# Token layers taken image by image, attention of one image beside the FFN of another

## The chip, the cores and the metric

The kernel runs on one core of one Trainium2 chip. The time is device microseconds (us) of an execution; four runs of the kernel before gave 10815.32 to 10830.81 us, median 10817.74. One further execution was recorded by the hardware profiler and is what the views of the profile show. Engines are named as the profile names them: PE (TensorE, matmuls and transposes; PEld is its weight load), DVE (VectorE), ACT (ScalarE), POOL (GpSimd), SP (SyncE, which issues the DMAs here). L684 is line 684 of the kernel.

## The reference

Four images of 64 x 64 pixels with 96 channels pass four layers. Layers 0 and 1 are group normalisation and a selective scan in four directions, added to x. Layers 2 and 3 treat the pixels as tokens, 4096 an image, and they are what the change rearranges:

```
t = t + attn(ln(t), Wqkv, bqkv, Wff, bff)     # layer 2, and again layer 3
t = t + ffn(ln(t), W1, b1, W2, b2)

attn(x):  q, k, v = split(x @ Wqkv + bqkv), 6 heads of 16
          y = (q @ k.T / 4) @ v               # per head, no softmax
          return y @ Wff + bff
ffn(x):   h = relu(qlinear(x, W1, b1))        # 96 -> 384
          return qlinear(h, W2, b2)           # 384 -> 96
qlinear(x, W, b) = qacc(qacc(q8(x) @ q8(W).T) + q8(b))
```

`ln` normalises each token over its 96 channels. `q8` rounds to an 8-bit float with 5 exponent and 2 mantissa bits, `qacc` to a 16-bit float. No image needs another one's data in any layer.

## The kernel before

**Scans.** A layer's four images are taken as two pairs; two layers give four units. Each unit is `scan_inputs` (projection and convolution), `scan_pair` (the selective scan, with its order written out by hand) and `scan_outputs`. `between_scans` drives the outputs of one unit and the inputs of the next in turn, as two generators; the outputs of the last unit run alone, since there is no next unit. `scan_outputs` is a loop of 16 steps, each for four groups of 128 tokens: load zt, ys and xr; statistics of ys and `ln_rs` (a power on POOL); normalise ys on ACT (L289); six transposes into the PSUM tile `pt` (L296); two ACT activations `gt<-pt` (L299); multiply by zt on DVE (L306); eight matmuls `po` (L310, L311); add xr and store x (L313, L316). `pt` and `po` have one buffer each.

**Token layers.** All four images are loaded to SBUF as `tok[b]`, tiles of 128 partitions x 32 tokens x 96 channels, and stay there. Then `attention` runs over the four images, `ffn` over the four, and both again for layer 3. Each function opens its own pools and loads its own weights at its start.

*The norm*, `token_norm`, opens both. DVE takes 32 statistics `tstats` (L684), five small operations make the variance, DVE adds epsilon (`tn_ve`, L79), POOL takes the power -0.5 of 128 x 32 values (`tn_rs`, L81), DVE makes `tshift` (L699). Then the normalised tokens `tn` are written, 24 of 32 by ACT (L705) and 8 by POOL (L703).

*Attention.* Having no softmax, it becomes one 97 x 96 matrix an image: PE sums the Gram matrix of tn with a column of ones (L754, 32 matmuls), and five small products with the weights, with DVE copies between them, give `whole` (L764). `turn_tokens` transposes tn in groups of four (`tnps`, L714), ACT copies them to `tnt`. Then for each of eight groups PE multiplies four blocks of tnt by `whole` (`ops`, L769) and DVE adds the result to the tokens (L771).

*FFN.* The same norm and turning (ACT's copy `xq` rounds to 8 bits), then eight chunks of 512 tokens. For each of three blocks of the hidden layer: a matmul `hps`, ACT copies to 16 bits (`h`, L811), DVE adds the bias and takes the maximum with 0 (`hb`, L813), POOL rounds to 8 bits (`hq`, L814). Then twelve matmuls `ops` (L818), ACT copies (`o`, L822), DVE adds the bias (`ob`, L824) and adds to the tokens (`tok`, L826). In layer 3 each image is stored to `out` at its end.

**The order of the work.** Scans are kept in program order. In the other parts the scheduler of the framework fixes the order on each engine when the program is built, from the program order, the dependences and the buffers of each pool (two as a rule, three for `hps`). Every engine and SP's queue then runs its instructions in that order, and one that waits holds up those behind it. The tokens are loaded from the DRAM tensor to which the outputs of the second scan layer store x.

Of the kernel before, what the change touches and what calls it, by code (L numbers as in the profile page):

```python
# [16 lines left out]
F32 = mybir.dt.float32  # L17
BF16 = mybir.dt.bfloat16
# [7 lines left out]
NB = 4  # L26
HW = 64
L = HW * HW
C = 96
# [74 lines left out]
def between_scans(tc, cst, ident, half, u, before, after):  # L104


    with ExitStack() as stage:
        if before is None:
            for _ in scan_inputs(tc, stage, cst, ident, half, u, *after):
                pass  # L110
        elif after is None:
            for _ in scan_outputs(tc, stage, ident, half, *before):
                pass
        else:
            ins = scan_inputs(tc, stage, cst, ident, half, u, *after)
            for _ in scan_outputs(tc, stage, ident, half, *before):
                for _ in range(2):
                    next(ins, None)
            for _ in ins:
                pass  # L120
# [126 lines left out]
def scan_outputs(tc, stage, ident, half, layer, pr):  # L247
# [4 lines left out]
    pp = stage.enter_context(tc.tile_pool(name="c_ps", bufs=1, space=PSUM))  # L252
# [3 lines left out]
    for g in range(NT // 2):  # L256
# [36 lines left out]
        pt = pp.tile([128, 3, 2, 128], F32, name="pt")  # L293
        for j, first in enumerate((0, 256, 128)):
            for t in range(2):
                nc.tensor.transpose(pt[:, j, t], ys[:, t, first : first + 128], ident)  # L296
        gt = p2.tile([128, 3, 2, 128], F32, name="gt")
        for s, js in ((0, slice(0, 2)), (1, slice(2, 3))):
            nc.scalar.activation(  # L299
                gt[:, js],  # L300
                pt[:, js],
                AF.Identity,
                bias=par[:, s, P_NB : P_NB + 1],
                scale=par[:, s, P_NW : P_NW + 1],
            )
        nc.vector.tensor_tensor(gt, gt, zt.rearrange("p j (t q) -> p j t q", q=128), ALU.mult)  # L306
        po = pp.tile([128, 2, 2, C], F32, name="po")
# [372 lines left out]
def token_norm(nc, pool, half, t, tn):  # L680

    stats = pool.tile([128, NT, 6], F32, name="tstats")
    for j in range(NT):
        nc.vector.bn_stats(stats[:, j], t[:, j])  # L684

# [13 lines left out]
    nc.vector.scalar_tensor_tensor(shift, mean2, -0.5, rs, ALU.mult, ALU.mult)  # L699
    for j in range(NT):  # L700
        scale, bias = rs[:, j : j + 1], shift[:, j : j + 1]
        if j % 4 == 3:
            nc.gpsimd.tensor_scalar(tn[:, j, :C], t[:, j], scale, bias, ALU.mult, ALU.add)  # L703
        else:
            nc.scalar.activation(tn[:, j, :C], t[:, j], AF.Identity, bias=bias, scale=scale)  # L705


def turn_tokens(nc, pp, ident, tn, out):

    n = tn.shape[2]  # L710
    for g in range(NT // 4):
        ps = pp.tile([n, 512], F32, name="tnps", tag="tp")
        for j in range(4):
            nc.tensor.transpose(ps[:, 128 * j : 128 * j + 128], tn[:, 4 * g + j], ident)  # L714
        nc.scalar.activation(out[:, 512 * g : 512 * g + 512], ps, AF.Copy, saturate=False)


def attention(tc, cst, ident, half, tok, w):


    nc = tc.nc
    with ExitStack() as stage:
        p1 = stage.enter_context(tc.tile_pool(name="t1", bufs=1))
        p2 = stage.enter_context(tc.tile_pool(name="t2", bufs=2))
        pp = stage.enter_context(tc.tile_pool(name="t_ps", bufs=2, space=PSUM))

        wkv = p1.tile([C + 1, 2 * C], F32, name="wkv")
        nc.sync.dma_start(out=wkv, in_=w["wkv"])
        wq = p1.tile([C, C + 1], F32, name="wq")
        nc.sync.dma_start(out=wq, in_=w["wq"])  # L730
        wff = p1.tile([C, C], F32, name="wff")
        nc.sync.dma_start(out=wff, in_=w["Wff"])
        bff = p1.tile([C + 1, C], F32, name="bff")
        nc.sync.dma_start(out=bff, in_=w["bff"])

        def product(a, b, name):

            ps = pp.tile([a.shape[1], b.shape[1]], F32, name=name, tag="small")
            nc.tensor.matmul(ps, a, b, start=True, stop=True)
            return ps  # L740

        def kept(ps, name):
            to = p2.tile(list(ps.shape), F32, name=name)
            nc.vector.tensor_copy(to, ps)
            return to

        for b in range(NB):
            t = tok[b]
            tn = p2.tile([128, NT, C + 1], F32, name="tn")
            nc.gpsimd.memset(tn[:, :, C : C + 1], 1.0)  # L750
            token_norm(nc, p2, half, t, tn)
            gram = pp.tile([C + 1, C + 1], F32, name="gram")
            for j in range(NT):
                nc.tensor.matmul(gram, tn[:, j], tn[:, j], start=(j == 0), stop=(j == NT - 1))  # L754
            tnt = p2.tile([C + 1, L], F32, name="tnt")
            turn_tokens(nc, pp, ident, tn, tnt)
            gk = kept(product(kept(gram, "gram"), wkv[:, :C], "gkps"), "gk")
            vk = product(wkv[:, C:], gk, "vkps")

            heads = p2.tile([C, C], F32, name="heads")  # L760
            nc.vector.tensor_tensor(heads, cst["heads"], vk, ALU.mult)
            rest = kept(product(heads, wff, "hps"), "rest")
            whole = p2.tile([C + 1, C], F32, name="whole")
            nc.vector.tensor_tensor(whole, bff, product(wq, rest, "wps"), ALU.add)  # L764
            for g in range(NT // 4):
                po = pp.tile([128, 4, C], F32, name="ops", tag="o")
                for j in range(4):
                    at = 512 * g + 128 * j
                    nc.tensor.matmul(po[:, j], tnt[:, at : at + 128], whole, start=True, stop=True)  # L769
                tg = t[:, 4 * g : 4 * g + 4]  # L770
                nc.vector.tensor_tensor(tg, tg, po, ALU.add)  # L771


def ffn(tc, ident, half, tok, w, out=None):

    nc = tc.nc
    NH = HID // 128
    with ExitStack() as stage:
        p1 = stage.enter_context(tc.tile_pool(name="f1", bufs=1))
        p2 = stage.enter_context(tc.tile_pool(name="f2", bufs=2))  # L780
        pp = stage.enter_context(tc.tile_pool(name="f_ps", bufs=2, space=PSUM))

        def quantised(shape, src, name, back=False):
            raw = p1.tile(shape, F32, name=name)
            nc.sync.dma_start(out=raw, in_=src)
            q = p1.tile(shape, E5M2, name=name + "q")
            nc.vector.tensor_copy(q, raw, saturate=False)
            if back:
                nc.vector.tensor_copy(raw, q)
                return raw  # L790
            return q

        w1 = quantised([C, HID], w["W1"], "w1")
        w2 = quantised([128, NH, C], w["W2"].rearrange("(k p) c -> p k c", p=128), "w2")
        b1 = quantised([128, NH], w["b1"], "b1", back=True)
        b2 = quantised([128, 1, C], w["b2"].unsqueeze(0).partition_broadcast(128), "b2", back=True)

        for b in range(NB):
            t = tok[b]
            tn = p2.tile([128, NT, C], F32, name="tn")  # L800
            token_norm(nc, p2, half, t, tn)
            xq = p2.tile([C, L], E5M2, name="xq")
            turn_tokens(nc, pp, ident, tn, xq)
            for c in range(L // 512):
                cols = slice(512 * c, 512 * c + 512)
                hq = p2.tile([128, NH, 512], E5M2, name="hq")
                for k in range(NH):
                    ps = pp.tile([128, 512], F32, name="hps", tag="mm", bufs=3)
                    nc.tensor.matmul(ps, w1[:, 128 * k : 128 * k + 128], xq[:, cols], start=True, stop=True)
                    h = p2.tile([128, 512], F16, name="h16")  # L810
                    nc.scalar.copy(h, ps)  # L811
                    hb = p2.tile([128, 512], F16, name="hb16")
                    nc.vector.tensor_scalar(hb, h, b1[:, k : k + 1], 0.0, ALU.add, ALU.max)  # L813
                    nc.gpsimd.tensor_copy(hq[:, k], hb, saturate=False)  # L814
                po = pp.tile([128, 4, C], F32, name="ops", tag="o")
                for j in range(4):
                    for k in range(NH):
                        nc.tensor.matmul(  # L818
                            po[:, j], hq[:, k, 128 * j : 128 * j + 128], w2[:, k], start=(k == 0), stop=(k == NH - 1)
                        )  # L820
# [6 lines left out]
            if out is not None:  # L827
                nc.sync.dma_start(out=out[b * L : (b + 1) * L, :].rearrange("(p j) c -> p j c", j=NT), in_=t)
# [164 lines left out]
```

## Time and profile before

| what | us |
|---|---|
| median of four runs | 10817.74 |
| profiled execution, its own time | 10834.03 |
| its span (first to last instruction) | 10832.2 |
| scans with the three stages between them, up to | 10137 |
| outputs of the last unit, alone | 10137 to 10263 (126) |
| attention, layer 2, four images | 10263 to 10377 (114) |
| FFN, layer 2 | 10377 to 10546 (169) |
| attention, layer 3 | 10546 to 10654 (108) |
| FFN, layer 3, with the last store | 10654 to 10832 (178) |

The profiled execution stands 0.15% above the median. Over the whole span DVE is busy 90%, POOL 83%, ACT 81% and PE 75% of the time, but that is an average over the scans, which fill 94% of it; the tail after 10137 us is 695 us with other limits. In the views, a line gives the start, the busy time, the engine, the line of the kernel, out<-in with shapes, how many instructions it joins, and in brackets the idle time before it and what ended that. The columns of a table by windows are the busy time of each engine (with the number of its instructions), the granted clock of PE as a share of full speed, the share of the DMA engines' time, and GB/s.

### The profile page before, as it was taken

The numbers are of one execution on the slowest core, as the hardware profiler recorded it, in microseconds if no ns is written. First come the engines' busy times: TensorE is split into PE (matmuls) and PEld (weight loads), VectorE is DVE, ScalarE is ACT, GpSimd is POOL, SyncE is SP. The second block draws the span as 40 slices with busy tenths as digits, with TensorE's granted clock in tenths as the row PEclk, the third lists the DMA queues.
The fourth block names the chain that finished last, engine by engine and source line by source line (L and its number), as shares of the span: only waits on it lengthen the run. The fifth ranks groups of instructions, "written<-read, shape, count | busy, mean of one in ns | idle before, by whom it ended". The sixth has DMA issues, their size and how long they took to land. (4 is left out here: it accounts for less than half of the span.)

```text
span 10832.2 us, 143079 instructions
## 1 busy us (share of the span) xinstructions
PE 8093.1 (75%) x48032; PEld 5988.3 (55%) x48032; DVE 9706.9 (90%) x6962; ACT 8760.8 (81%) x18679; POOL 9006.5 (83%) x5242
## 2 busy tenths in 40 slices
PE   7777777777777777776877777777777777777666
PEld 4555555554555555555555555555455555555544
DVE  7999999997999999998799999999699999999655
ACT  6888888885888888886688888888588888888556
POOL 3999999992899999996598999999299999999544
PEclk9889899888899888988898999988888989898766
DMA  4677777775677777777576777777467777777600
GB/s 124 205 209 214 214 224 216 215 219 141 201 209 211 217 214 217 218 214 194 149 210 207 214 218 220 220 216 216 134 206 210 213 215 221 219 215 214 185 3 25
DMA packets 960471, 2114.16 MB, mean 195 GB/s; under 512 B 413526, under 2 KB 704664, under 8 KB 762008
## 3 DMA queue, kind: packets, MB, share of 16 engines
q1 hardware_dynamic: 959736, 2105.01, 68.0%
q8 instruction: 381, 6.24, 0.3%
q14 instruction: 354, 2.90, 0.1%
HBM read 1943.27 MB, written 161.48 MB: 194 GB/s over the span
## 5 line engine op out<-in xcount | busy, mean ns | idle before, releaser
L71 POOL TENSOR_TENSOR h<-h,cb 128x1024 f32<-128x1024 f32 x3072 | 7201.2, 2368 | 277.7 <-issue 77.2
L71 DVE TENSOR_TENSOR_SCAN h<-da,last,bp 128x1024 f32<-128x1024 f32 x2064 | 4735.1, 2334 | 131.7 <-PE bp L71 14.4
L71 ACT ACTIVATE x<-dut,bt 128x128 f32<-128x128 f32 x12288 | 3494.9, 369 | 1.8 <-PE bp L71 1.2
L71 PE MATMUL yp<-ident,h 128*128 128x128 f32 x24576 | 3343.0, 296 | 9.8 <-POOL h L71 9.8
L71 PEld LDWEIGHTS yp<-ident,h 128*128 128x128 f32 x24576 | 3170.2, 156 | 127.7 <-issue 77.2
L71 ACT ACTIVATE da<-delta,amat 128x1024 f32<-128x1024 f32 x2752 | 3063.6, 1138 | 183.4 <-DVE h L71 183.0
L71 PE MATMUL bp<-ident,x 128*128 128x128 f32 x10240 | 1655.7, 313 | 1305.9 <-DVE h L71 928.6
L71 PEld LDWEIGHTS bp<-ident,x 128*128 128x128 f32 x10240 | 1338.2, 161 | 1859.0 <-ACT x L71 1045.0
L71 DVE TENSOR_TENSOR bp<-du,bp 128x1024 f32<-128x1024 f32 x1472 | 1778.6, 1212 | 244.2 <-PE bp L71 242.5
L71 DVE TENSOR_TENSOR_SCAN h<-da,bp 128x1024 f32<-128x1024 f32 x688 | 1537.5, 2274 | 48.1 <-ACT da L71 8.5
L71 PE MATMUL bp<-bparts,sel 96*128 96x512 bf16 x2944 | 921.1, 395 | 839.8 <-DVE h L71 816.2
L71 PEld LDWEIGHTS <-sel 96*128 96x128 bf16 x2944 | 224.7, 100 | 1648.7 <-DVE h L71 1037.4
L71 ACT ACTIVATE bp<-delta,amat 128x1024 f32<-128x1024 f32 x320 | 358.1, 1119 | 542.3 <-DVE h L71 540.7
L71 POOL TENSOR_TENSOR dbu<-du,bb 128x1024 f32<-128x1024 f32 x320 | 755.9, 2362 | 0.0
L71 POOL TENSOR_TENSOR du<-delta,u 128x1024 f32<-128x1024 f32 x192 | 506.7, 2639 | 199.6 <-ACT delta L71 172.7
L81 POOL TENSOR_TENSOR ln_rs<-ln_ve,half 128x4 f32<-128x4 f32 x64 | 84.0, 1312 | 594.4 <-DVE ln_ve L79 494.3
L71 DVE TENSOR_TENSOR_SCAN h<-bp,last,dbu 128x1024 f32<-128x1024 f32 x240 | 558.4, 2327 | 13.4 <-POOL dbu L71 12.3
L71 PE MATMUL xps<-u,wx 128*76 128x512 f32 x768 | 559.5, 818 | 5.7 <-ACT cdt L71 2.9
L71 POOL COPY last<-h 128x2 f32<-128x2 f32 x1152 | 225.2, 195 | 401.1 <-DVE h L71 398.4
L71 ACT ACT_TABLE_LOAD x384 | 492.7, 1283 | 6.9
L71 PE MATMUL dps<-cdt,wdt 12*128 12x512 f32 x768 | 450.2, 667 | 0.0
L71 ACT COPY dut<-dups 128x512 f32<-128x512 f32 x384 | 220.8, 575 | 251.6 <-PE dups L71 251.6
(132 smaller groups left out, 6444.9 us busy)
## 6 DMA issues: line engine op xcount, KB each, us to landing
cb<-crow SPq DMA_DIRECT2D x1024, 1024.0 KB
cb<-crow SPq DMA_DIRECT2D x1024, 512.0 KB
bb<-crow SPq DMA_DIRECT2D x384, 256.0 KB
bb<-crow SPq DMA_DIRECT2D x128, 512.0 KB
y<-ysum SPq DMA_DIRECT2D x192, 256.0 KB
kept<-y SPq DMA_DIRECT2D x160, 256.0 KB
y<-ysum SPq DMA_DIRECT2D x64, 512.0 KB
zt<-zg SPq DMA_DIRECT2D x64, 384.0 KB
```

Of the source, the lines that this page charges most:

```text
L71: return self.tc.keep_in_program_order(getattr(self.engine, op)(*args, **kwargs))
L81: nc.gpsimd.tensor_tensor(rs, ve, half, ALU.pow)
```

## The change

The pools of the token layers are opened once, in a new function `token_layers`, which also drives the last unit's `scan_outputs`. `attention` and `ffn` become generators for one image, with a `yield` after every eight statistics, after the norm, after every eight tn and after every group or chunk; the turning of tokens is done group by group, inside the loops. `together` advances its pieces one `yield` each in turn. The order of the pieces is written out: the last outputs with the first image's layer-2 attention; seven stages of one FFN and one attention of different images; the last FFN alone. All weights of both layers are loaded ahead of the last outputs, `tok0` and `tok1` too, `tok2` and `tok3` after them.

PSUM is shared out anew: Gram and the small products have one bank each (two before), `hps` two (three before), and the outputs use the banks of `hps` and `ops`. In `scan_outputs`, at every one of its four uses, `pt` becomes two tiles of three transposes, in two buffers, and `gt` takes four activations instead of two, half as wide. `sel` and `ident16` move to a pool that ends with the scans, so that their load stands behind the load of the layers' parameters.

```
-        pt = pp.tile([128, 3, 2, 128], F32, name="pt")
-        for j, first in enumerate((0, 256, 128)):
-            for t in range(2):
-                nc.tensor.transpose(pt[:, j, t], ys[:, t, first : first + 128], ident)
         gt = p2.tile([128, 3, 2, 128], F32, name="gt")
-        for s, js in ((0, slice(0, 2)), (1, slice(2, 3))):
-            nc.scalar.activation(gt[:, js], pt[:, js], AF.Identity, ...)
+        for t in range(2):
+            pt = pp.tile([128, 3, 128], F32, name="pt", tag=turned)
+            for j, first in enumerate((0, 256, 128)):
+                nc.tensor.transpose(pt[:, j], ys[:, t, first : first + 128], ident)
+            for s, js in ((0, slice(0, 2)), (1, slice(2, 3))):
+                nc.scalar.activation(gt[:, js, t], pt[:, js], AF.Identity, ...)
...
     for j in range(NT):
         nc.vector.bn_stats(stats[:, j], t[:, j])
+        if j % 8 == 7:
+            yield
...
     nc.vector.scalar_tensor_tensor(shift, mean2, -0.5, rs, ALU.mult, ALU.mult)
+    yield
     for j in range(NT):
...
+        if j % 8 == 7:
+            yield
...
+def attention(nc, pool, pp, cst, ident, half, t, w):
...
+    tn = pool.tile([128, NT, C + 1], F32, name="tn", bufs=3)
+    nc.gpsimd.memset(tn[:, :, C : C + 1], 1.0)
+    yield from token_norm(nc, pool, half, t, tn)
+    gram = pp.tile([C + 1, C + 1], F32, name="gram", bufs=1)
+    tnt = pool.tile([C + 1, L], F32, name="tnt")
     for g in range(NT // 4):
+        for j in range(4 * g, 4 * g + 4):
+            nc.tensor.matmul(gram, tn[:, j], tn[:, j], start=(j == 0), stop=(j == NT - 1))
+        turn_tokens(nc, pp, ident, tn, g, tnt)
+        yield
...
+def ffn(nc, pool, pp, ident, half, t, w, out=None):
...
+    tn = pool.tile([128, NT, C + 1], F32, name="tn", bufs=3)
+    yield from token_norm(nc, pool, half, t, tn)
+    xq = pool.tile([C, L], E5M2, name="xq")
+    for c in range(L // 512):
+        turn_tokens(nc, pp, ident, tn, c, xq)
+        yield
...
+        yield
...
+def token_layers(tc, cst, ident, half, x, outputs, a):
...
+        load(0)
+        load(1)
+        wa = [weights(attention_weights, n, ("wq", "wkv", "Wff", "bff")) for n in (2, 3)]
+        wf = [weights(ffn_weights, n, ("W1", "b1", "W2", "b2")) for n in (2, 3)]
...
+        def together(*pieces):
+            pieces = list(pieces)
+            while pieces:
+                for one in list(pieces):
+                    if next(one, pieces) is pieces:
+                        pieces.remove(one)
+
+        together(scan_outputs(tc, stage, ident, half, *outputs, pp, "mm", "o"), attend(0, 0))
+        load(2)
+        load(3)
+        together(feed(0, 0), attend(0, 1))
+        together(attend(1, 0), feed(0, 1))
+        together(feed(1, 0), attend(1, 1))
+        together(feed(1, 1), attend(0, 2))
+        together(feed(0, 2), attend(0, 3))
+        together(attend(1, 2), feed(0, 3))
+        together(feed(1, 2), attend(1, 3))
+        together(feed(1, 3))
```

## The prediction

> **What bounds the kernel now.** I read the windows of the tail first, since the scans before 10137 us keep their order, then the timeline inside one stage of each kind. Windows by stage (busy us of each engine, granted PE clock, DMA share, GB/s): last outputs; attention, FFN of layer 2; attention, FFN of layer 3.
>
> ```profile
> core 0: us, PE busy (x) PEld busy (x) DVE busy (x) ACT busy (x) POOL busy (x), PEclk, DMA share, GB/s
> 10137.00:10263.00 126.00, 72.78 (x353) 60.66 (x352) 52.27 (x192) 50.42 (x97) 16.12 (x16) 0.69 0.60 164
> 10263.00:10377.00 114.00, 83.55 (x672) 81.78 (x672) 50.18 (x227) 51.72 (x128) 35.20 (x40) 0.78 0.13 50
> 10377.00:10546.00 169.00, 100.38 (x608) 55.31 (x608) 106.90 (x304) 116.48 (x256) 106.69 (x132) 0.60 0.00 1
> 10546.00:10654.00 108.00, 82.50 (x672) 80.66 (x672) 47.88 (x213) 51.73 (x128) 35.20 (x40) 0.80 0.01 3
> 10654.00:10832.00 178.00, 99.36 (x608) 55.47 (x608) 110.14 (x320) 116.39 (x256) 106.73 (x132) 0.61 0.09 38
> ```
>
> No engine is busy over 75% of a stage: the tail is chains with engines waiting, 569 us for eight (attention, FFN) pairs of one image, 71.1 us a pair. Engine time that could lie beside other time is there. What matters is which stretches the new order lays side by side. The norm that opens each attention and FFN, in the timeline (start, us, engine):
>
> ```profile
> 10266.30 5.36 DVE L684 BATCH_NORM_STATS2 tstats<-tok 128x6 f32<-128x96 f32 x33 [3.05 <-DMA x<-xo]
> ...
> 10272.88 5.43 POOL L81 TENSOR_TENSOR tn_rs<-tn_ve,half 128x32 f32<-128x32 f32 x1 [6.18 <-DVE tn_ve L79]
> ...
> 10278.70 8.70 ACT L705 ACTIVATE tn<-tok,tshift,tn_rs 128x96 f32<-128x96 f32 x24 [20.10 <-DVE tshift L699]
> ```
>
> A norm is a chain over three engines: statistics, a power, the writing of tn. Before, most norms lie beside the previous image's main part. The main part of an FFN, VectorE alone:
>
> ```profile
> 10800.55 0.35 DVE L813 TENSOR_SCALAR hb<-h,b 128x512 f16<-128x512 f16 x1 [9.29 <-ACT h L811]
> ...
> 10812.13 0.54 DVE L826 TENSOR_TENSOR tok<-tok,ob 128x384 f32<-128x384 f32 x1
> 10812.59 0.95 DVE L813 TENSOR_SCALAR hb<-h,b 128x512 f16<-128x512 f16 x2
> 10813.65 0.78 DVE L824 TENSOR_TENSOR ob<-o,b 128x384 f16<-128x384 f16 x1
> 10814.35 0.70 DVE L813 TENSOR_SCALAR hb<-h,b 128x512 f16<-128x512 f16 x1
> 10814.97 0.54 DVE L826 TENSOR_TENSOR tok<-tok,ob 128x384 f32<-128x384 f32 x1
> ...
> 10825.61 0.56 DVE L826 TENSOR_TENSOR tok<-tok,ob 128x384 f32<-128x384 f32 x1
> ```
>
> One chunk of 512 tokens takes 2.84 us (tok at 10812.13 and 10814.97) with VectorE hardly idle: what attention adds there to VectorE comes on top. The clock, on attention's 16-matmul groups of two images:
>
> ```profile
> 10303.38 3.73 PE L769 MATMUL ops<-whole,tnt 97*128 97x96 f32 x16 [3.90 <-DVE whole L764]
> ...
> 10333.96 1.95 PE L769 MATMUL ops<-whole,tnt 97*128 97x96 f32 x16
> ```
>
> The same work takes 3.73 or 1.95 us. Last, the outputs loop, 6.85 us a step (10177.68 to 10184.53), a chain PE, ScalarE, VectorE:
>
> ```profile
> 10177.68 0.46 PE L310 MATMUL po<-wo,gt 128*128 128x96 f32 x2 [2.38 <-DVE gt L306]
> ...
> 10180.45 1.70 PE L296 MATMUL pt<-ident,ys 128*128 128x128 f32 x6
> ...
> 10182.25 1.23 ACT L299 ACTIVATE gt<-pt,par 128x512 f32<-128x512 f32 x2 [0.99 <-PE pt L296]
> 10183.52 0.96 DVE L306 TENSOR_TENSOR gt<-gt,zt 128x768 f32<-128x768 f32 x1 [1.00 <-ACT gt L299]
> 10184.53 0.46 PE L310 MATMUL po<-wo,gt 128*128 128x96 f32 x2 [2.38 <-DVE gt L306]
> ```
>
> **Part 1, outputs beside the first attention.** In the built order, token loads and 16 weight loads stand on SP ahead of the first zt load, and the whole first norm ahead of the first ys activation on ScalarE. SP: y stores end 10140.7, 16 issues of about 0.45 us (as zt's 0.48) put zt at about 10148.5, from 10143.25; hidden, because ScalarE is later. VectorE: 32 statistics (5.2 us), quantising copies and small operations bring tn_ve to about 10150.4; pow 5.43; 20 of ScalarE's tn at 8.70/24 = 0.3625 us, 7.3; with latencies first ys is at about 10163.6 against 10151.33: +12.3. In the 16 steps, attention's Gram, transposes, copies and products (PE about 25 us cold) share the engines: at worst 18, at best 0, as PE is busy 73 of 126 us. I take 10, the loop being a chain through PE. Turning in two halves lets ScalarE start after three transposes instead of six, but takes four activations for two: about -0.3 a step, -5 (0 to -10). The loop ends at 10263.3 + 12.3 + 10 - 5 = 10280.6. Attention's last eight adds stand behind the last po: 7 us (0.98 to 1.15 + 0.55 each with cold PE, some already covered). First pair stage: T0 = 10288 (10277 to 10300).
>
> **Part 2, seven pair stages.** The two pieces are driven step by step in turn, so both norms run at the same time and nothing of a main part is beside them. The built order shows it: between the last tok add of one stage and the first transposed copy of the next, VectorE has 35 to 54 (mean 47.7) of the 64 statistics, POOL two pows in a row, and ScalarE all 48 tn ahead of anything else. Priced:
> - statistics 47.7 x 0.163 (5.36/33) = 7.8
> - twelve small operations and tn_ve, six of which take about 1.0 in a norm: 1.5
> - two pows at 5.44: 10.9; tshift 0.35
> - ScalarE has written six tn beside the second pow; 42 x 0.3625 = 15.2; latency 0.1
>
> Norms: 35.8 us a stage. Their work equals before's; only its cover is gone.
>
> The main part, last tn to last tok add. First hb after about 2.0 us (xq copy 0.56, hps 0.63, h 0.56, latency). Lower pace, VectorE's: first hb to last add 25.6 (10800.55 to 10826.2), eight attention adds at 0.5 = 4.0, some 16 statistics of the next stage 2.6: 34.2. Upper, PE cold: each of eight chunks 2.4 for the FFN (three hps at 0.42, twelve ops at about 1.0 to 1.2), 1.06 for each of two sets of four transposes, 0.93 for attention's ops (3.73/4): 43.6, less 4 of transposes beside the tn writing, plus 2.0 in front and 2 behind: 43.6. Which? Rows with a clock near these stages': PE would be busy about 184/4 = 46 of 75 us, 61%, like FFN's 59% at 0.60, not attention's 73% at 0.78; but transposes and groups in a row opened it in attention. I take the middle, 38.9.
>
> The rule: the Trainium skill, "TensorE: Matmul & The Clock Gate", Part 1, says the array opens to full clock after some 3.4 us of sustained work and falls back after an idle window. By it the main part would be cold only at its start, VectorE would set the pace, and the sum below would come to about 10821. The row at 10303.38 speaks otherwise: three more groups follow at 3.62 us without a gap, up to 10318, about 15 us cold; the measurement decides, so I do not take the rule's value.
>
> P = 35.8 + 38.9 = 74.7 us a pair, against 71.1. The other edits in the pairs (one bank less for Gram, small and hps, weights loaded early) cost 0: two hps still let PE run ahead of h at 0.56, and if that cover goes, each chunk waits up to 0.4 for ScalarE, 3 us a stage, inside the cold bound. The out store of each image stands on SP beside other stages' work; no issue waits behind it.
>
> **Part 3, the last FFN alone.** Norm: 22 statistics of 32 left, 3.6; small 1.15; pow 5.44; tshift 0.35; 24 tn 8.7: 19.2. Main: 10795.1 (last tn) to 10826.2 = 31.1, less the 3.4 by which the first hb now comes sooner, its transposes no longer all ahead: 27.7. The store 6.0 as before (10826.2 to 10832.2).
>
> **Part 4, between the scans.** Three stages with the outputs' four activations, PE, VectorE and ScalarE about 97% busy there (2560 to 2600 us): 16 steps x 3 x about 0.5 us of ScalarE = 24, against the -0.3 x 48 = -14 of the earlier start; +4 (-14 to +24, the likely part -6 to +12). Scans: no instruction moves, 0; sel's load stands behind par's but is first used in the scan.
>
> **Sum.** 10288 + 7 x 74.7 + (19.2 + 27.7) + 6.0 + 4 = 10867.8 of span, +35.6 to 10832.2. The profiled execution took 10834.03, 16 above the median of 10817.74: carried over, 10853.
>
> **Rivals.**
> - *VectorE's pace (no change).* The denser stage opens the clock and main is 34.2: P = 70.0, span 10835, median 10820. For: attention's groups at 1.95. Against: FFN stages at 0.60.
> - *PE cold throughout.* Main 43.6, P = 79.4: span 10901, median 10886. For: the 15 us cold. Against: 0.78 in attention.
> - *Faster: attention rides in the gaps of VectorE.* If hb at 0.70 is slow only through POOL's hq beside it and the new spacing thins that out, the adds and statistics cost nothing and main is 2.0 + 25.6 = 27.6: P = 63.4, span 10789, median 10774. It decides from a main under 33.8, where 7 P = 487. Against: VectorE has no gap in the chunk above.
> - *The norms overlap after all*, the engines running ahead of each other: each us off the 35.8 is 7 us; it would need 5 us a stage to break even. The orders on ScalarE and POOL speak against it.
>
> **How the numbers follow.** A measurement here tells about 0.2% (21.6 us) from no change. Forecast 0.48; cold 0.19; VectorE's pace 0.19; the gaps or overlapping norms 0.14. Slower takes the forecast, the cold case and a little of VectorE's pace with T0 and the between stages at their upper bounds (12 + 8); same the rest of that and some mild overlap; faster most of the last. Range: from the early side of the gaps (main near 31.5, 10802) to the cold case with 7 us of T0's bound on it, 10893. The likeliest alone: 10835 to 10875.
>
> **What would show it.** Stages about 75 us from last tok add to last tok add; about 36 us of each without hb; two tn_rs in a row; ScalarE 48 tn in a row; first ys about 12 us later; outputs ending near 10281; main parts 35 to 43 us at a clock of 0.6 to 0.7. Wrong if a norm shows hb beside it, if main is under 34, or if the between stages move by over 15 us.

## The result and the profile after

The changed kernel takes 10847.02 us (median of 32 runs, 10830.53 to 10863.15), the kernel before, run beside it, 10824.09 us (50 runs). The ratio is 1.0021 with a 95% interval of 1.0016 to 1.0026: slower by 0.21%, 23 us.

The end of the last scan wanders by some 10 us either way from one profile to the next, though no scan instruction differs. So I compare the **tail**, from the end of POOL's last multiplication by cb (10135.86 us in the profile before, 10130.00 after) to the end of the span: 696.3 us before, 714.6 after, +18.3. The other 5 us of the +23 are not in this tail; ahead of it the kernels differ in the edit of pt between the scans and in the later load of sel and ident16, and two profiles can't show so little there.

The changed kernel's windows: last outputs with the first attention, and that attention's last adds; then, for two pair stages (an FFN and an attention driven together), the norms and the main parts (all that follows the norms); then the last FFN's norm and main part. Columns are the busy us of each engine with its instructions, the granted PE clock, DMA share and GB/s.

```profile
core 0: us, PE busy (x) PEld busy (x) DVE busy (x) ACT busy (x) POOL busy (x), PEclk, DMA share, GB/s
10130.00:10276.00 146.00, 82.73 (x471) 75.18 (x471) 61.47 (x248) 70.44 (x161) 25.86 (x27) 0.72 0.57 159
10276.00:10289.00 13.00, 12.55 (x59) 12.31 (x58) 6.06 (x18) 0.00 (x0) 0.00 (x0) 0.50 0.68 255
10289.00:10325.00 36.00, 12.74 (x65) 11.18 (x66) 10.67 (x69) 17.18 (x48) 17.39 (x19) 0.50 0.00 2
10325.00:10362.00 37.00, 30.55 (x257) 23.18 (x256) 28.48 (x82) 24.66 (x49) 16.50 (x24) 0.94 0.00 1
...
10432.00:10468.00 36.00, 12.73 (x65) 11.18 (x66) 10.51 (x67) 17.18 (x48) 17.43 (x19) 0.50 0.00 0
10468.00:10503.00 35.00, 29.11 (x257) 22.09 (x256) 25.68 (x63) 24.64 (x49) 17.02 (x24) 0.98 0.00 1
...
10790.00:10811.00 21.00, 3.50 (x12) 1.79 (x13) 4.98 (x30) 10.08 (x27) 8.66 (x9) 0.59 0.18 76
10811.00:10844.00 33.00, 19.59 (x142) 10.77 (x140) 22.03 (x40) 19.34 (x38) 16.89 (x24) 0.71 0.12 48
```

A stage falls in two halves. In the norms no engine is busy half of the 36 us; in the main part PE works at a clock of 0.94 and 0.98 and is busy over 80% of the time. The timeline of the changed kernel (start, us, engine, line), first where the last outputs start, then from the end of the first attention to the first main part:

```profile
10141.00 4.73 DVE L679 BATCH_NORM_STATS2 tstats<-tok 128x6 f32<-128x96 f32 x29 [13.64 <-DMA wq<-in_l_wq]
...
10150.58 0.36 DVE L776 CAST w1q<-w 96x384 fp8e5<-96x384 f32 x1 [4.86 <-DMA w<-in_l_W]
...
10152.63 5.43 POOL L81 TENSOR_TENSOR tn_rs<-tn_ve,half 128x32 f32<-128x32 f32 x1 [11.61 <-DVE tn_ve L79]
...
10158.37 7.27 ACT L703 ACTIVATE tn<-tok,tshift,tn_rs 128x96 f32<-128x96 f32 x20 [26.18 <-DMA zt<-zg]
...
10165.55 1.85 ACT L284 ACTIVATE ys<-ys,shift,ln_rs 128x192 f32<-128x192 f32 x4
...
10274.69 13.86 PE L763 MATMUL ops<-whole,tnt 97*128 97x96 f32 x64
...
10288.59 0.56 DVE L765 TENSOR_TENSOR tok<-tok,ops 128x384 f32<-128x384 f32 x1 [0.82 <-PE ops L763]
10289.06 8.71 DVE L679 BATCH_NORM_STATS2 tstats<-tok 128x6 f32<-128x96 f32 x54
...
10299.00 10.82 POOL L81 TENSOR_TENSOR tn_rs<-tn_ve,half 128x32 f32<-128x32 f32 x2 [32.97 <-DVE tn_ve L79]
...
10310.07 15.14 ACT L703 ACTIVATE tn<-tok,tshift,tn_rs 128x96 f32<-128x96 f32 x42 [3.09 <-DVE tshift L696]
...
10325.12 0.57 ACT L714 ACTIVATE xq<-tnps 96x512 fp8e5<-96x512 f32 x1
...
10327.55 1.18 DVE L809 TENSOR_SCALAR hb<-h,b 128x512 f16<-128x512 f16 x2 [0.78 <-ACT h L807]
```

At the start, the statistics of the first attention stop after 29 of 32, because a quantising copy stands next in VectorE's order and waits 4.86 us for its weight; the outputs' first ys waits behind the whole norm. Then the norms of the first pair: statistics, two powers, 42 tn, one behind the other. From the last add (ending 10289.15) to the first copy are 36 us in which no hb runs.

### The profile page after: what moved, and what is told of

Same layout as the page of the kernel before. It is cut to its first block, busy times and chain, and to the rows that moved or that the text cites. A ratio compares the mean times of both kernels' runs of the same rounds, so it can differ in the third digit from the quotient of the medians.

```text
span 10844.6 us, 143249 instructions
## 1 busy us (share of the span) xinstructions
PE 8058.5 (74%) x48032; PEld 5968.1 (55%) x48032; DVE 9683.7 (89%) x6962; ACT 8785.7 (81%) x18807; POOL 8997.4 (83%) x5242
## 4 chain that ended last, share of the span: by engine, by line
ACT 36%; DVE 20%; issue 19%; PE 18%; POOL 5%; DMA 1%; SPq 0%; DVEq 0%; POOLq 0%; ACTq 0%
ACT x L71 16%; ACT da L71 13%; DVE h L71 11%; PE yp L71 6%; DVE bp L71 5%; PE bp L71 5%; POOL h L71 3%; ACT bp L71 2%; PE xps L71 2%; DVE u L166 2%; PE dps L71 1%; ACT L71 1%; ACT tn L703 1%; PE cps L150 1%; PE dups L71 1%
## 5 line engine op out<-in xcount | busy, mean ns | idle before, releaser
L71 DVE TENSOR_TENSOR_SCAN h<-da,last,bp 128x1024 f32<-128x1024 f32 x2064 | 4735.1, 2334 | 130.4 <-PE bp L71 13.2
```

What stands on the lines that cost most here:

```text
L71: return self.tc.keep_in_program_order(getattr(self.engine, op)(*args, **kwargs))
```

## The experiments

The theory going in: the norms in lockstep (both at the same time, step by step) leave half of each stage bare, with no other work beside them, and whatever covers or shortens them comes off the time. The rivals: main parts and norms together would use up the engines, or the waits would only move. "To the changed kernel" below is against its 10847; each ratio is against the kernel before on the same chip.

| run | median us | ratio (95%) | tail us |
|---|---|---|---|
| kernel before | 10824.09 | 1 | 696.3 |
| changed kernel | 10847.02 | 1.0021 (1.0016 to 1.0026) | 714.6 |
| e1 split pt alone | 10830.68 | 1.0006 (0.9997 to 1.0015) | 697.4 |
| e2 offset | 10803.41 | 0.9982 (0.9973 to 0.9991) | 670.8 |
| e3 no ob | 10827.62 | 0.9998 (0.9989 to 1.0008) | 695.4 |
| e4 fewer ops | 10841.56 | 1.0016 (1.0006 to 1.0025) | 701.3 |
| e5 weights late | 10836.18 | 1.0009 (1.0000 to 1.0019) | 700.7 |
| e6 same order | 10850.57 | 1.0023 (1.0014 to 1.0032) | 711.0 |
| e7 four streams | 10788.68 | 0.9965 (0.9953 to 0.9978) | 649.6 |
| e8 power in pieces | 10839.56 | 1.0012 (1.0003 to 1.0021) | 700.5 |
| e9 square root | 10780.04 | 0.9957 (0.9945 to 0.9970) | 636.8 |
| e10 four, square root | 10682.29 | 0.9864 (0.9849 to 0.9879) | 550.3 |
| e11 before, square root | 10746.38 | 0.9929 (0.9917 to 0.9942) | 615.5 |
| e12 outputs first | 10853.12 | 1.0025 (1.0015 to 1.0036) | 724.6 |

**e1, the split of pt alone,** on the kernel before: the hunk of the change in `scan_outputs`, with two buffers for pt.

> The kernel before with the one edit of pt alone: two tiles of three transposes in two buffers, four gt activations instead of two, in all four uses of the outputs. My step 4 (+4 us in the three between stages, bounds -14 to +24) and the -5 in the last outputs: -1 us together, 10820 to 10832 at a median of 10824 for the kernel before, with the last outputs' step at about 6.5 instead of 6.85 us. Rival, read off the profiles where the scans of the changed kernel end 5.9 us earlier: the edit gains about 2 us in each between stage, and 11 us in all, 10813.

Measured 10830.68, +0.06% with an interval from -0.03 to +0.15%. The rival's -11 us falls; +4 between the scans fits, but is too small to be shown by this run alone. First ys to the end of the last xo takes 110.5 us, 111.9 before: the earlier start of gt is worth 0.1 us a step, not 0.3.

**e2, an offset of half a piece.** The pairs of the changed kernel as two streams:

```
-        together(feed(0, 0), attend(0, 1))
-        together(attend(1, 0), feed(0, 1))
...
+        offset(
+            (0, chain((feed, 0, 0), (attend, 1, 0), (feed, 1, 0), (attend, 0, 2), ...)),
+            (13, chain((attend, 0, 1), (feed, 0, 1), (attend, 1, 1), (feed, 1, 1), ...)),
+        )
```

> The changed kernel with the same pieces in the same pairs, but the second stream starts 13 yields (half a piece) after the first, so that the norm of one lies beside the main part of the other. Theory (the norms in lockstep leave 36 us of each 71.6 us stage uncovered): half a stage becomes one norm of 20 us beside a main part of 28 to 30, a stage 60, so 7 x 11.6 = 81 us less than the changed kernel, about 10770 (10735 to 10800). Rival (the engines are used up when main parts and norms lie together, or each waits in the other's order): 10830 or more.

Measured 10803.41, 44 us less than the changed kernel and less than the kernel before too: covering the norms pays, about half of the 81 worked out, and just short of the theory's bound of 10800. The timeline of this run, POOL, shows a wait that can have taken the other half:

```profile
10417.98 0.61 POOL L810 CAST hq<-hb 128x512 fp8e5<-128x512 f16 x1 [0.44 <-DVE tvar L693]
10418.78 5.43 POOL L81 TENSOR_TENSOR tn_rs<-tn_ve,half 128x32 f32<-128x32 f32 x1 [0.19 <-DVE tn_ve L79]
10424.15 0.61 POOL L810 CAST hq<-hb 128x512 fp8e5<-128x512 f16 x1
```

and VectorE:

```profile
10418.80 0.25 DVE L679 BATCH_NORM_STATS2 tstats<-tok 128x6 f32<-128x96 f32 x1
10424.24 0.57 DVE L696 SCALAR_TENSOR_TENSOR tshift<-tmean,tn_rs 128x32 f32<-128x32 f32 x1 [5.19 <-POOL tn_rs L81]
10424.73 0.34 DVE L809 TENSOR_SCALAR hb<-h,b 128x512 f16<-128x512 f16 x1
```

The power stands in POOL's order between two hq, and VectorE stands still for tshift with an hb behind it. The norm of one image stops the main part of the other for 5 us; VectorE waited 77.8 us like this in 14 norms (first table of e8). PE was hardly slower than in the changed kernel: busy 310.46 us for 2299 matmuls from 10305 to 10790 us, against 297.15 us for 2240 in its seven pair stages. How much of the missing half the wait is, this run doesn't show.

**e3 and e4, what sets the pace of the main parts.** e3:

```
...
-        nc.vector.tensor_tensor(ob, o, b2.to_broadcast([128, 4, C]), ALU.add)
...
-        nc.vector.tensor_tensor(tg, tg, ob, ALU.add)
+        nc.vector.tensor_tensor(tg, tg, o, ALU.add)
```

> The changed kernel without the bias of the second FFN product: ob is left out and VectorE adds o to the tokens, 0.54 us less on VectorE a chunk, 64 chunks. If VectorE sets the pace of the main parts: -0.54 x 8 = -4.3 us a stage, -34 us in all, 10813. If PE or ScalarE sets it: under 10 us, 10837 to 10847.

e4:

```
-            for k in range(nh):
+            for k in range(nh - 1):
...
```

> The changed kernel with the second FFN product over two of the three hidden blocks (the third is left out): 8 matmuls instead of 12 a chunk, 0.2 us less on PE at the open clock, 0.33 when cold. If PE sets the pace of the main parts: -13 to -21 us in all, 10826 to 10834. If VectorE sets it: no change within 5 us.

e3 gained 19 us of tail (median -19), e4 13 (median -5, its interval overlaps that of the changed kernel, so its gain rests on the tail). A stage, from the first power of one to that of the next, went from 70.9 to 68.6 and 69.2 us. Over the seven pair stages VectorE's busy time fell from 256.11 us to 233.00 in e3, 3.3 a stage (the add that is left takes a little longer), and brought 2.3; PE's fell from 297.15 to 279.06 in e4, 2.6 a stage, and brought 1.7. In each case about two thirds of the time taken from the engine come off. Both theories fall in their pure form: work of both engines enters the time of a stage, not the pace of one alone.

**e5, the weights behind the outputs.**

```
-        wa = [weights(attention_weights, n, ("wq", "wkv", "Wff", "bff")) for n in (2, 3)]
-        wf = [weights(ffn_weights, n, ("W1", "b1", "W2", "b2")) for n in (2, 3)]
+        wa, wf = [weights(attention_weights, 2, ("wq", "wkv", "Wff", "bff"))], []
...
         together(scan_outputs(tc, stage, ident, half, *outputs, pp, "mm", "o"), attend(0, 0))
+        wa.append(weights(attention_weights, 3, ("wq", "wkv", "Wff", "bff")))
+        wf.extend(weights(ffn_weights, n, ("W1", "b1", "W2", "b2")) for n in (2, 3))
```

> The changed kernel with only layer 2's attention weights loaded ahead of the last outputs; the other twelve weight loads and their quantising copies stand behind the outputs. In the changed kernel the first ys activation comes 34.4 us after the scan's last copy starts, 20 later than before; zt is issued at 10151.5 and VectorE waits 4.86 us for an FFN weight ahead of the last statistics. Theory (the weights cost 8 of these 20 us): first ys 7 to 12 us sooner and the end with it, 10837 at a median of 10847 for the changed kernel. Rival (the loop is held by something else, or the loads come back at the first FFN): under 3 us.

Measured 10836.18 and 13.9 us less tail: the first ys comes 20.5 us after the scan's end instead of 35.6, and all but 1 of these 15 reach the end. As in the theory, and more. But the edit moved more than loads. In the changed kernel 20 tn stand ahead of the first ys on ScalarE (the line at 10158.37 above); here the scheduler put ys first:

```profile
10149.22 1.86 ACT L284 ACTIVATE ys<-ys,shift,ln_rs 128x192 f32<-128x192 f32 x4 [18.34 <-DVE tn_ve L79]
...
10155.00 1.54 ACT L703 ACTIVATE tn<-tok,tshift,tn_rs 128x96 f32<-128x96 f32 x4 [2.22 <-DVE tshift L696]
```

So the 15 us belong to the moved weights and the new order together; this run does not part the two.

**e6, the outputs driven alone, then the attention.**

```
-        together(scan_outputs(tc, stage, ident, half, *outputs, pp, "mm", "o"), attend(0, 0))
+        together(scan_outputs(tc, stage, ident, half, *outputs, pp, "mm", "o"))
+        together(attend(0, 0))
```

> The changed kernel with the last outputs alone and the first image's attention after them. Outputs about 20 us sooner (first ys as before, less what the weights ahead of zt cost), 14 us of the attention's adds no longer behind them as such, but a norm of 20 and a main part of about 33 alone: +19 to +27 us to the changed kernel, 10866 to 10874, if laying the attention beside the outputs is worth what the trace suggests. Rival (the late start of the outputs eats it): within 5 us of 10847.

It told nothing of the overlap. From the end of the scans on, the order of instructions on PE, VectorE, ScalarE and POOL came out the same as in the changed kernel: the order in which the two pieces are written did not matter to the scheduler here. It is a second measurement of nearly the same program, 10850.57, tail 711.0; these two tails agree to 4 us.

**e7, four streams,** each 13 yields behind the other, the first beside the outputs:

```
+        offset(
+            (0, scan_outputs(tc, stage, ident, half, *outputs, pp, "mm", "o")),
+            (0, chain((attend, 0, 0), (feed, 0, 0), (attend, 1, 0), (feed, 1, 0))),
+            (13, chain((attend, 0, 1), (feed, 0, 1), (attend, 1, 1), (feed, 1, 1))),
+            (26, chain((load2, 0, 2), (attend, 0, 2), (feed, 0, 2), (attend, 1, 2), (feed, 1, 2))),
+            (39, chain((load2, 0, 3), (attend, 0, 3), (feed, 0, 3), (attend, 1, 3), (feed, 1, 3))),
+        )
```

> The four images as four streams, each its own attention, FFN, attention, FFN, each starting 13 yields (half a piece) after the one before, the first beside the last outputs (tiles of the pieces in three or four buffers to allow it). At any time about two main parts and one or two norms run. If uncovered norms are what the tail loses, the stages go to the engines' own time, ScalarE 42 and VectorE 39 us a pair plus about 11 of waits for the power: 10650 to 10700. Rival (VectorE and POOL wait in order for the 5.4 us power, and everything behind them, as in the run with the offset, where VectorE waited 78 us for it): 10760 or more.

Measured 10788.68: 15 us faster than e2, but with the rival's size. More work side by side brings little while the power is there: VectorE waited 75.1 us for it in 14 norms from 10300 to 10770 us.

**e8, the power in four pieces,** on e2:

```
...
+    nc.vector.tensor_scalar(mean2, mean2, -0.5, None, ALU.mult)
+    for j in range(0, NT, 8):
+        js = slice(j, j + 8)
+        nc.gpsimd.tensor_tensor(rs[:, js], ve[:, js], half[:, js], ALU.pow)
+        nc.gpsimd.tensor_tensor(shift[:, js], mean2[:, js], rs[:, js], ALU.mult)
+        yield
```

> The run with the offset, and the power in four pieces of 8 columns with a yield after each, tshift on POOL behind each piece (mean prepared on VectorE), so that no VectorE instruction waits for the power and hq of the other image goes between the pieces. In the run with the offset VectorE waited 77.8 us for tn_rs in 14 norms, and PE 136 us for hq. Theory (these waits are what kept the offset at -44 instead of -81): 45 to 80 us less than its 10803, 10725 to 10760. Rival (the waits lay beside other work): within 15 us of 10803.

A miss, by more than either said: 10839.56, 36 us slower than e2. Waits by engine and line, what they waited for, us in total, times, longest; e2 first, from 10320 to 10790 us:

```profile
POOL hq L810 <- DVE hb L809: 99.5, 120, 7.7
DVE tshift L696 <- POOL tn_rs L81: 77.8, 14, 8.9
ACT o L818 <- PE ops L814: 27.1, 32, 6.8
DVE hb L809 <- POOL hq L810: 11.0, 13, 3.5
```

and e8, from 10305 to 10800 us:

```profile
POOL hq L814 <- DVE hb L813: 146.0, 112, 14.7
PE ops L818 <- POOL hq L814: 105.2, 95, 9.6
ACT o L822 <- PE ops L818: 74.1, 35, 10.1
DVE hb L813 <- POOL hq L814: 62.0, 26, 9.8
```

VectorE no longer waits for the power, but most pieces still run together on POOL (a norm's four pieces as 6.4 us in a row in most norms), and hq waits behind them and the products for tshift. The wait went from VectorE into the chain hb, hq, ops, o. POOL also had more to do: 64 pieces of 1.68 us, 107 us, where 16 powers took 87, and 64 products of 0.21 us. That points at the power's place on POOL, not at the one instruction that waits for it, but this run does not part the place from the added work; the next three runs take the power off POOL.

**e9, a square root in place of the power,** on the changed kernel:

```
+    if tag == "tn":
+        sd = pool.tile(shape, F32, name="tn_sd")
+        nc.scalar.activation(sd, ve, AF.Sqrt)
+        nc.vector.reciprocal(rs, sd)
+        return rs
     nc.gpsimd.tensor_tensor(rs, ve, half, ALU.pow)
```

> The changed kernel with the power of the token norms replaced by a square root on ScalarE (128 x 32) and a reciprocal on VectorE. In every pair stage two powers of 5.44 us stand in a row on POOL with nothing beside them. Theory (the norms of a stage are a bare chain, so what goes out of the chain goes out of the time): -10.9 + about 1.0 a stage, seven stages, -4.9 + 0.5 for the last FFN and the first attention each: -75 to -80, 10767 to 10775 at 10847 for the changed kernel; loading another function table on ScalarE, if it is needed, gives back 1.3 to 2.6 a stage. Rival (the time of the chain is taken up again by ScalarE's 48 tn or the main parts): less than 30 gained, 10817 or more.

Its timeline for the first pair of norms:

```profile
10287.33 8.71 DVE L684 BATCH_NORM_STATS2 tstats<-tok 128x6 f32<-128x96 f32 x54
...
10297.23 0.56 ACT L83 ACTIVATE tn_sd<-tn_ve 128x32 f32<-128x32 f32 x2 [22.25 <-DVE tn_ve L79]
10297.49 0.68 DVE L84 RECIPROCAL tn_rs<-tn_sd 128x32 f32<-128x32 f32 x2
...
10298.25 17.29 ACT L708 ACTIVATE tn<-tok,tshift,tn_rs 128x96 f32<-128x96 f32 x48 [0.47 <-DVE tshift L701]
```

Two powers of 10.8 have become 1.0 us. The tail is 77.8 us shorter (75 to 80 expected): seven stages 8.5 each, the first attention 13.2, the last FFN 4.9. The median is 67 less, 5 short of the expected range; in this profile the scans ended 11 us later than in that of the changed kernel. Most of what leaves the bare chain leaves the time. A stage gives 8.5 of the 9.9 forecast, since ScalarE now writes 48 tn in a row, 17.29 us, where it wrote six of them beside the second power. That the tail still meets the forecast is luck: the first attention gave 13.2 where 4.4 were expected, 5.1 of it by an earlier first ys and 6.5 between the last xo and the first pair stage.

**e11, the same on the kernel before.**

> The kernel before with the same square root in the token norms. There only the first image's norm of each of the four passes stands bare, the others lie beside main parts: 4 x -4.9 + 0.5 = -18 to -20, 10805 at 10825. So the same edit should be worth four times as much in the changed kernel. Rival (the power blocks hq in the FFN passes too, three times a pass, so the edit is worth the same in both kernels): -50 or more.

Measured 10746.38, -0.71%, 81 us of tail: the rival's size. By passes, last add to last add: the first image of layer 2's attention 55.7 to 34.5, its other three 55.0 to 51.6, FFN 172.7 to 156.9, attention 107.0 to 82.5, FFN 172.6 to 156.5. So the rival's reason, the FFN passes, covers 32 of the 81; the other 49 come from the attention passes. I had read the kernel before as covering all norms but four. Its VectorE in the first attention shows otherwise:

```profile
10278.34 0.19 DVE L699 SCALAR_TENSOR_TENSOR tshift<-tmean,tn_rs 128x32 f32<-128x32 f32 x1 [5.22 <-POOL tn_rs L81]
...
10289.53 0.19 DVE L699 SCALAR_TENSOR_TENSOR tshift<-tmean,tn_rs 128x32 f32<-128x32 f32 x1 [5.22 <-POOL tn_rs L81]
...
10302.01 0.19 DVE L699 SCALAR_TENSOR_TENSOR tshift<-tmean,tn_rs 128x32 f32<-128x32 f32 x1 [4.79 <-POOL tn_rs L81]
...
10303.09 0.23 DVE L764 TENSOR_TENSOR whole<-bff,wps 97x96 f32<-97x96 f32 x1
```

Three norms stand ahead of the first image's `whole`, and VectorE stands still about 5 us in each: `whole` comes at 10303. With the square root it comes 25.7 us after the end of the last xo instead of 39.8. Along with this PE became faster: in layer 3's attention pass its granted clock went from 0.80 to 0.92 and its busy time from 82.50 to 72.90 us, for the same 672 matmuls. How much of the 24.5 us there comes by the clock is not shown.

**e12, the outputs in a stage of their own,** before the pools of the tokens are opened:

```
+        with ExitStack() as first:
+            po = first.enter_context(tc.tile_pool(name="c_ps", bufs=2, space=PSUM))
+            for _ in scan_outputs(tc, first, ident, half, *outputs, po):
+                pass
...
-        together(scan_outputs(tc, stage, ident, half, *outputs, pp, "mm", "o"), attend(0, 0))
+        together(attend(0, 0))
```

> The changed kernel with the last outputs in a stage of their own, whose buffers are given free before the tokens and weights are loaded, so that the first attention can't start beside them (in e6 the scheduler built nearly the same program as the changed kernel, so it told nothing of this). First ys 14 us after the scan's end instead of 34, outputs ending about 126 after it instead of 145, then the token load, a norm of 20 and a main part of 33: 182 against 159 us from the scan's end to the first pair stage. If that is so, laying the attention beside the outputs is worth 23 us: 10870. Rival (worth nothing): within 6 of 10847.

```profile
10252.67 0.55 DVE L308 TENSOR_TENSOR xo<-xr,po 128x384 f32<-128x384 f32 x1 [3.82 <-PE po L306]
10262.45 5.20 DVE L679 BATCH_NORM_STATS2 tstats<-tok 128x6 f32<-128x96 f32 x32 [9.23 <-DMA tok<-x]
...
10296.36 0.55 DVE L765 TENSOR_TENSOR tok<-tok,ops 128x384 f32<-128x384 f32 x1
```

The outputs end 127 us after the scan (10126.03), as expected, and the first pair stage starts 170.9 after it instead of 159.2: the overlap is worth 12 us in the profiles, half of the 23, and 6 in the medians, which alone do not tell it from nothing. The attention alone took 34 us from its first statistic, not the 53 I had put down. What the overlap costs is the late start, of which e5 took 15 us.

**e10, four streams, the square root, late weights.**

> The four streams with the square root, and twelve of the sixteen weight loads behind the outputs. Theory (what holds the four streams at 10789 is the power on POOL, which VectorE's tshift and POOL's hq wait for: 16 norms of about 5): 80 to 100 us below 10789, 10690 to 10710. Rival (as with the power in pieces, the wait moves on to the next engine in order): above 10750.

Measured 10682.29, ratio 0.9864 (0.9849 to 0.9879): 1.4% faster than the kernel before, 0.6% faster than e11. Against e7 it is 106 us, a little over the 80 to 100 expected; the late weights are in it, which e5 priced at 11 to 14. Its windows, over the stretch with all streams and over the end:

```profile
core 0: us, PE busy (x) PEld busy (x) DVE busy (x) ACT busy (x) POOL busy (x), PEclk, DMA share, GB/s
...
10287.00:10640.00 353.00, 275.43 (x2081) 213.28 (x2081) 240.04 (x839) 274.54 (x651) 158.54 (x273) 0.87 0.03 10
10640.00:10687.00 47.00, 25.11 (x191) 14.22 (x191) 26.62 (x51) 31.60 (x68) 24.55 (x37) 0.72 0.16 68
```

PE and ScalarE are busy 78% of the 353 us at a clock of 0.87; in e7 the clock was 0.76 from 10300 to 10750 us. That is what image-wise order brings here once norms lie beside main parts, no power stands in a queue that main parts use and the weights are out of the way. It changes three things against the changed kernel; e5, e7 and e9 show each of them by itself to be a gain.

## Why the prediction was right, and where it was off

10853 was forecast, slower, from 10817.74; 10847 came, from 10824.09: a change of +23, where the sum said +35.6. The sign and the reason hold; the size was half too large, and that the predicted time came within 6 us is luck, because the median before moved up by 6. Term by term, in the profiles:

| term | predicted us | measured us |
|---|---|---|
| scan's end to first ys | 27.7 | 35.6 |
| first ys to the end of the last xo | 117.0 | 109.9 |
| from there to the first pair stage | 7.4 | 13.7 |
| norms of a pair stage (mean of 7) | 35.8 | 35.2 |
| main part of a pair stage | 38.9 | 36.4 |
| last FFN | 46.9 | 48.2 |
| last store | 6.0 | 6.1 |
| tail | 727.9 | 714.6 |

- **The norms.** Right to 0.6 us a stage, and shown to be the loss from both sides: an offset gained 44 us, a shorter chain 67 to 78. Two powers in a row, no hb in the norms and ScalarE's tn in one run stand in the profile as forecast.
- **The main part** is the step that failed: "Rows with a clock near these stages'" put PE near FFN's 0.60, and "I take the middle, 38.9". The clock in the seven main parts was 0.87 to 0.98. The 2.5 us a stage, 17.5 in all, are more than the whole difference of 13.3 in the tail; the norms add 4 to it and the other terms give 8 back. The no-change rival had the clock right but not the pace: 36.4 lies above VectorE's 34.2, and in e3 and e4 the work of both engines enters the time. The rule that I weighed (the Trainium skill, "TensorE: Matmul & The Clock Gate", Part 1) gave a sum nearer to the mains than the row of the first attention did. It does not explain both: the 64 ops in a row at 10274.69, in the windows and the timeline of the changed kernel above, kept PE busy for 13.86 us, and the clock granted there was 0.50.
- **The outputs.** Three errors that nearly cancel. I priced a weight load on SP like a zt load, 0.45 us; wkv and wq took 1.5 to 2.3, all sixteen 15.5 where the price gave 7.2, and VectorE waited for a weight in the middle of the statistics (+8). The loop did not suffer from the attention beside it: 109.9, 2 less than before (-7). And the attention's eight adds stood whole behind the last po, 64 matmuls at a clock of 0.50 (+6).
- **Between the scans,** +4: the +23 of the medians less the +18.3 of the tail leaves 4.6, and e1 does not contradict it. Not shown by itself.
- **The rival on the other side,** attention in VectorE's gaps at a main part of 27.6, is out by 9 us a stage. **PE cold throughout** (a clock near 0.5) is out by 7. **The norms overlap after all** did not happen; that they can, and what it is worth, is e2.
- **Two readings** were a little off, and no term of the sum was sized by them: PE was busy 76% of layer 3's attention, not under 75% in every stage, and from 2560 to 2600 us VectorE and ScalarE were busy 94 to 95%, only PE 97%.

What I did not see in the profile before: the power on POOL holds up VectorE there too; replacing it is worth 81 us (e11). I took those norms as hidden, so I compared a bare norm with one at no cost. That error does not enter the sum, which was made from stage times, but it kept me from naming the power as the thing to remove.

## What to carry to other kernels

Two pieces that are driven in lockstep meet phase by phase: if both open with the same chain, the chains lie side by side and their main parts too, and nothing is covered; start one half a piece later, and look at the built order, since a scheduler may ignore what the program's order suggests (e6) or change it with an edit elsewhere (e5). Before covering a chain, look for the long instruction in it that sits in a queue that the covering work needs: replacing one 5.4 us instruction, which runs 16 times, was worth 67 us in one kernel and 80 in the other, covering its chain by an offset 44, and the new order paid most with both and late weights, 144 under the kernel before. Compare stages from a common mark, not whole spans, when the part ahead of them wanders by more than the effect.

## What the runs showed of the hardware

- The same reciprocal square root of 128 x 32 values takes 5.43 us as a power on POOL (four pieces of 8 columns 6.4), and 0.23 us on ScalarE with 0.35 on VectorE as square root and reciprocal; one table load of 1.28 us for the whole tail, as the other functions there needed no other.
- The clock of PE in these stages went to 0.87 to 0.98 within main parts that leave PE idle 15 to 18% of the time, and stayed at 0.50 for 13.86 us of matmuls without a gap. What opens it in the one and not in the other was not tried.
- In a chain through four engines, about two thirds of the busy time taken from one of them came off the time of a stage: 2.3 of VectorE's 3.3 us (e3), 1.7 of PE's 2.6 (e4).
